# Input statistics, the conv's last chunk and a split inverse in a hand-ordered WKV and graph-conv kernel

## The chip, the cores and the metric

The kernel runs on one core of one Trainium2 chip. The time is the device time of one launch in microseconds (us), given as the median of the runs. Each engine of a core (TensorE, VectorE, ScalarE, GpSimd, and SyncE, which here only issues DMAs) works through its own queue in order. Engines wait for one another through semaphores.

## The reference

The input x has 16 images of 192 channels and 56 x 56 = 3136 positions, in float32. Three WKV layers and a graph convolution follow one another. Each takes the group norm of x (32 groups) and adds its result to x.

```python
def _L0_conv_ref(x, Wk, Wv, Wr, Wo, ln_g, ln_b, w_decay, u):
    k, v, r = xs @ Wk.T, xs @ Wv.T, xs @ Wr.T            # over positions t
    x_fwd = wkv_scan(-exp(w_decay), u, k, v)
    x_bwd = flip(wkv_scan(-exp(w_decay), u, flip(k), flip(v)))
    h = sigmoid(r) * 0.5 * (x_fwd + x_bwd)
    h = (h - mean(h)) * rsqrt(var(h) + 1e-5) * ln_g + ln_b   # over channels
    return h @ Wo.T
def _L3_conv_ref(x, conv_w, ...):
    x_j = max(roll(x, +-2, rows) - x, roll(x, +-2, columns) - x, 0)
    y = conv_w @ concat([x, x_j]) + conv_b
    return gelu(batch_norm(y))
for layer in (L0, L1, L2, L3): x = x + layer(_gn(x))
```

(The code above is shortened. The scan is a quotient of two decaying sums along t, one weighted by exp(k) and one by exp(k) times v, with a bonus u for the current position.)

## The kernel before, in words

**Tiles.** Two images make a pair, and there are 8 pairs. A pair's 2 x 192 channels are laid on 128 partitions as three rows j = 0, 2, 1 (two full ones and one that holds 64 channels of each image), which the kernel always takes in this order. The 3136 positions are cut into 7 chunks of 448 columns. So a tile is 128 x 3 x 448, most operations come in three instructions of 128x448, and operations on a whole tile have 1344 columns. All these tiles live in 33 slots of SBUF. A slot that is given back goes to the end of a list, and the next one is taken from its front (`Slot`, L501 to L509). A slot that was given back a moment ago may still have a reader under way, and its next writer then waits for it. [...]

**Units of work.** A WKV layer of a pair has 7 forward units A (chunks 0 to 6) and then 7 backward units B (chunks 6 to 0). A conv of a pair has 7 units C.
- A: product k (`a_keys`) and its exponential into `ek` (`a_exp`); product v (`a_values`); `ekv` = v times ek (`a_ekv`, L908); a scan of ek into `den` (`a_q`) and of ekv into `h` (`a_p`), each three instructions at L855; the bonus terms `a_den` and `a_num` (L870, one instruction of 896 columns and one of 448); the inverse of den as exp(-ln(den)) on ScalarE (`ln` L933, `exp_minus` L936); and `a_y` (L940), GpSimd's product of h with it, after which den's slot is given back. For chunks 0 and 6, `a_y` ends with small products into `chk` (L946, L948).
- B: product r (`b_gate`), exponential (`b_exp`) and sigmoid; backward scans `b_q` and `b_p`; `b_den`, `b_num`; the inverse; nine GpSimd products and sums (`b_mix`, L996 to L998); squares (L1005), sums over channels on TensorE (`b_sums`), the row of deviations (`b_rs1`, `b_rs2`, `b_rs3`), its spread over the partitions (`b_spread`, L1036), `b_scale` (L1041), the output product (`b_out`), the sum with x (`b_x`, L1054) and its store, and the statistics of the new x for the next group norm (`b_stats`).
- C: maxima over rows and columns on VectorE (`c_rows`, `c_columns`, L1080 to L1096), products of x and of the maxima (`c_product`, halves 0 and 1, "cv" in the profile), and Gelu with two table loads, sum and store (`c_end`, `store`).
- Z: statistics of a pair's input, needed by its first layer's norm: two ScalarE instructions per row (L724, L725; each is followed by a read of the accumulator), six per chunk (`chunk_stats`).

**Order.** All engines' queues are written out by hand. Pairs go in two streams (even and odd). A list of 249 steps (L1165 to L1200), numbered from 0 here, puts the B units of one stream beside A or C units of the other. In the list's third column stands the Z unit of a step. Functions by kind of step issue the instructions: `both_a` (B beside A), `both_a_first` (the same, in the first step of six), `both_c` (B beside C), `forward_a` and `forward_c` (one unit alone), and `backward_alone`. What a B unit still has to do after its step is remembered in `late` as a stage (0, 0.5, 1, 2), and the next steps pick it up. Unfinished group norms are four parts in `norms`; each `gap()` issues one.

The stretches that the text speaks of are these:
- Steps 0 to 6 are pair 0's A units alone. Steps 8 to 13 have B of pair 0 beside A of pair 1, and step 14 is A6 alone.
- From step 15 on, layers alternate in the same way (B6 alone, six steps of both, A6 alone, 8 steps in all) up to the conv.
- Steps 48 to 53 are `both_c` (B of pair 1's last layer beside C of pair 0). Then comes a **lone stretch**: A0 of pair 2, C6 of pair 0, A1 to A6 of pair 2 (steps 54 to 61). There are six of these, in steps 54 to 61, 69 to 76, 116 to 123, 131 to 138, 178 to 185 and 193 to 200.

Before, Z units of pair p + 1 are counted in the steps in which pair p's first layer runs forward (L1203 to L1205). These are steps 0 to 6 for pair 1, steps 8 to 14 for pair 2, and the first five lone stretches for pairs 3 to 7. The chunk is loaded at the step's start, and its six ScalarE instructions stand at the step's end.

Of the kernel before, what the change touches and what calls it, by code (L numbers as in the profile page):

```python
# [34 lines left out]
F32 = mybir.dt.float32  # L35
# [438 lines left out]
def fast_path(ctx: ExitStack, tc: tile.TileContext, flag, x, wproj, wfold, wcfold, wconst, wgroup, sums, picks, vecs, out):  # L474
# [9 lines left out]
    small = ctx.enter_context(tc.tile_pool(name="fsmall", bufs=4))  # L484
    dram = ctx.enter_context(tc.tile_pool(name="fdram", bufs=1, space=bass.MemoryType.DRAM))
# [220 lines left out]
    class Run:  # L706
        def __init__(self, pr, l, stats, src=None, first=None):
            self.pr, self.l, self.stats, self.src = pr, l, stats, src
            self.xa, self.xb, self.xz = {}, {}, {}
            if first is not None:  # L710
                self.xa[0] = first
            self.begun, self.before = False, None
            self.bias, self.ps = {}, {}
            self.ek, self.ekv, self.h, self.den, self.sg, self.rs = {}, {}, {}, {}, {}, {}
            self.m, self.ml, self.q, self.p = {}, {}, {}, {}

    def new_stats():
        return small.tile([P, 2, 3, NL], F32, tag="stats", name=name("stats"))

    def chunk_stats(stats, xt, c, whole=False):  # L720

        for j in ORDER:
            if not whole:
                S.activation(junk, xt[:, j, :], AF.Identity, accum_out=stats[:, 0, j, c : c + 1])  # L724
            S.activation(junk, xt[:, j, :], AF.Square, accum_out=stats[:, 1, j, c : c + 1])  # L725
# [154 lines left out]

    def a_keys(run, c):
        product(run, "k", run.w[0], run.xa[c], c == 0)
        slot_of(run.ek, c, "ek")
        if c == 0:
            take_bias(run, "k", S)

    def a_exp(run, c, js):
        ps, e = run.ps["k"], run.ek[c]
        for j in js:
            S.activation(e.t[:, j, :], ps[j][:, 0:L], AF.Exp, bias=run.bias["k"][:, j, :])  # L890
            release(ps[j])

    def a_values(run, c):
        xs = run.xa.pop(c)
        product(run, "v", run.w[1], xs, c == 0)
        if c == NL - 1:

            run.xb[c] = xs
            mean_column(run, xs)
        else:  # L900
            xs.give()
# [9 lines left out]
    def a_q(run, c):  # L911
        run.den[c] = scan(run, "q", run.ek[c], AHEAD, c == 0)

    def a_save(run, c):
        if c < NL - 1:
            save(run.den[c], AHEAD, slot_of(run.ek, c + 1, "ek"), S)
        else:
            run.last = stile("cvb")
            S.activation(run.last, run.den[c].t[:, :, L - 1 : L], AF.Copy)  # L919
# [6 lines left out]
    def a_den(run, c):  # L926
        bonus(run, run.den[c], run.ek[c], run.den[c])

    def a_num(run, c):
        bonus(run, run.h[c], run.ekv[c], run.h[c])  # L930

    def ln(s):
        S.activation(s.t, s.t, AF.Ln)  # L933

    def exp_minus(s):
        S.activation(s.t, s.t, AF.Exp, scale=-1.0)  # L936

    def a_y(run, c):
        den = run.den.pop(c)
        G.tensor_mul(run.h[c].t, run.h[c].t, den.t)  # L940
        den.give()
        if c in (0, NL - 1):
            edge, grow = params[run.l][2:4]
            chk = run.chk[:, 3 * NL : 3 * NL + 9].rearrange("p (k j o) -> p k j o", k=3, o=1)
            col = 0 if c == 0 else L - 1
            G.tensor_mul(chk[:, 1 if c == 0 else 2], run.ek[c].t[:, :, col : col + 1], edge)  # L946
            if c == NL - 1:
                G.tensor_mul(chk[:, 0], run.last, grow)  # L948

# [195 lines left out]
    def z_stats(run, c):  # L1145
        xs = run.xz.pop(c)
        chunk_stats(run.stats, xs.t, c)
        xs.give()
# [3 lines left out]
    for pr in range(npairs):  # L1152
        runs = [Run(pr, 0, new_stats() if pr < 2 else None)]
        for l in range(NLAYERS):
            runs[-1].follow = Run(pr, l + 1, None)
            runs[-1].follow.before = runs[-1]
            runs[-1].dst = [dram.tile([P, 3, L], F32, tag=f"x{pr}_{l}_{c}", name=name("xd")) for c in range(NL)]
            runs.append(runs[-1].follow)
        chains.append(runs)
# [43 lines left out]
    for pr in range(1, npairs):  # L1203
        for c in range(NL):
            steps[at[pr - 1, 0, c]][2] = ("Z", chains[pr][0], c)  # L1205
    starts = {}
    for pr in range(npairs):
        counted = at[pr - 1, 0, NL - 1] + 1 if pr > 0 else 0
        starts.setdefault(max(counted, at[pr, 0, 0] - 2), []).append(chains[pr][0])
# [16 lines left out]
    def deviation(u):  # L1226
        b_rs1(*u)
        b_rs2(*u)
        b_rs3(*u)
        late[u] = 1  # L1230
# [26 lines left out]
    def both_a(b, a, nback, nfront):  # L1257
# [19 lines left out]
        invert(b[0].ek[b[1]])  # L1277
# [13 lines left out]
        a_save(*a)  # L1291
        exp_keys(nfront, (0, 2))
        b_squares(*b, (2,))
        exp_keys(nfront, (1,))
        b_squares(*b, (1,))
        b_sums(*b)
        a_p(*a, S)
        gap()
# [53 lines left out]
    def both_c(b, a, nback, nfront):  # L1352
# [45 lines left out]
        if l0:  # L1398
            spread_and_scale(l0)
        c_end(*a, False)  # L1400
        late[b] = 0

    def forward_a(a, nback, nfront):
# [5 lines left out]
        ahead = nfront is not None and nfront[1].begun  # L1409
        if ahead:  # L1410
            load_ahead(nfront)
# [3 lines left out]
        if l:  # L1415
# [12 lines left out]
            if ahead:  # L1428
                keys(nfront)
                exp_keys(nfront)  # L1430
# [4 lines left out]
            gap()  # L1435
        else:
            if l2:
                add(l2)
            if ahead:
                keys(nfront)  # L1440
            a_ekv(*a)
            if ahead:
                exp_keys(nfront)
            a_p(*a, S)
            if l0:
                squares_and_sums(l0)
                b_rs1(*l0)
                late[l0] = 0.5
            a_den(*a)
            invert(den())  # L1450
            a_num(*a)
            gap()
# [6 lines left out]
        if not ahead:  # L1459
            load_ahead(nfront)  # L1460
            keys(nfront)
            exp_keys(nfront)

    def forward_c(a, nback, nfront):
# [3 lines left out]
        if ahead:  # L1468
            load_ahead(nfront)
        c_product(*a, 0)  # L1470
        c_rows(*a)
        if h:
            b_rs2(*h)
            b_rs3(*h)
        c_columns(*a)
        store()
        if h:
            b_spread(*h)
            b_scale(*h)
# [66 lines left out]
    with tc.manual_schedule(engines={PE.engine, V.engine, S.engine, G.engine, nc.sync.engine}):  # L1546
# [6 lines left out]
        for i, (b, f, z) in enumerate(steps):  # L1553
# [6 lines left out]
            if z is not None:  # L1560
                if z[1].stats is None:
                    z[1].stats = new_stats()
# [3 lines left out]
            if f and not b and i + 2 < len(steps):  # L1566
                if nfront is not None and nfront[0] == "A" and steps[i + 2][1] is not None:
                    far = steps[i + 2][1]
                    if far[1] is nfront[1]:
                        load_ahead(far)  # L1570
            if b and f and f[0] == "A":
                (both_a if of_stage(0) is None else both_a_first)(b[1:], f[1:], nback, nfront)
            elif b and f:
                both_c(b[1:], f[1:], nback, nfront)
            elif f:
                (forward_a if f[0] == "A" else forward_c)(f[1:], nback, nfront)
# [7 lines left out]
        assert not late and not unsummed  # L1584
# [98 lines left out]
```

## Time and profile before

| what | value |
|---|---|
| median of 3 runs (lowest, highest) | 5327.02 us (5325.39, 5331.32) |
| profiled execution's own time | 5330.99 us |
| its span | 5329.2 us |
| granted TensorE clock in it | 0.919 |
| DVE busy | 4891.2 us (92%) |
| PE busy | 4607.2 us (86%) |
| ACT busy | 3701.4 us (69%) |
| POOL busy | 2750.7 us (52%) |
| an ordinary step of both halves (429.5 to 454.5) | 25.0 us, DVE busy 24.94 |
| a lone stretch with Z (1259.8 to 1388.3) | 128.5 us, DVE busy 98.4 |

The profile calls the engines PE (TensorE's matmuls), PEld (its weight loads), DVE (VectorE), ACT (ScalarE), POOL (GpSimd) and SPq (SyncE's queue of DMA issues). A busy PE is not a PE at its peak. A step's time is read on DVE, from the end of its last bonus term to that of the next step. A group or a timeline line is named by the tiles that it writes and reads ("p<-p,q": h from h and den; buffer names are those of the scans, so h appears as p and den as q).

### The profile page before, as it was taken

What the parts mean: (1) busy time and instruction counts of PE and PEld (TensorE: products, weight loads), DVE (VectorE), ACT (ScalarE), POOL (GpSimd) and SP (SyncE); (2) the same over time, 40 slices, a digit from 0 to 9 for tenths busy, and PEclk for the clock granted to TensorE, in tenths of its full rate; (3) what the DMA queues carried; (4) which work ended last, traced back from release to release, by engine and by line L of the source; (5) the groups of instructions that cost most, each with busy time, mean ns of one, the idle gap of its engine ahead of it and who ended that gap; (6) DMA issues with size and microseconds to landing.
All of it is one profiled execution on the core that took longest, in us unless ns stands there. A gap on an engine that the chain in (4) does not pass through costs nothing.

```text
span 5329.2 us, 51050 instructions
## 1 busy us (share of the span) xinstructions
PE 4607.2 (86%) x15206; PEld 1484.5 (28%) x15206; DVE 4891.2 (92%) x6460; ACT 3701.4 (69%) x7114; POOL 2750.7 (52%) x2109
## 2 busy tenths in 40 slices
PE   6789988988788898898888889988888888898897
PEld 2222222222222222222222222222222322232222
DVE  6799999997989999999797999999979799999995
ACT  6777777766766777777676777777757567777672
POOL 1455555654454565555354456555635355565562
PEclk8889999989899999999889999999998999999898
DMA  5222222134233222123424221222343312122233
GB/s 150 78 75 78 85 77 78 68 101 134 82 117 96 77 80 77 70 78 121 130 79 136 70 75 68 86 75 81 114 124 104 98 57 75 66 82 80 78 107 112
DMA packets 314270, 482.41 MB, mean 91 GB/s; under 512 B 66432, under 2 KB 306688, under 8 KB 313984
## 3 DMA queue, kind: packets, MB, share of 16 engines
q1 hardware_dynamic: 312832, 477.59, 28.1%
q8 instruction: 123, 2.02, 0.2%
q10 hardware_dynamic: 1152, 1.48, 0.1%
q14 instruction: 163, 1.34, 0.1%
HBM read 324.83 MB, written 154.14 MB: 90 GB/s over the span
## 4 chain that ended last, share of the span: by engine, by line
DVE 52%; PE 28%; ACT 7%; POOL 6%; issue 5%; DMA 2%; SPq 0%; DVEq 0%; POOLq 0%; ACTq 0%
DVE p L855 13%; DVE q L855 10%; DVE q L870 5%; DVE ek L870 4%; DVE ekv L908 3%; DVE p L1041 3%; DVE p L870 3%; DVE ekv L870 3%; DVE x L1054 2%; PE ops L592 2%; PE st L1014 2%; PE ops L594 2%; PE ops L593 2%; PE rsb L1036 2%; POOL p L998 2%
## 5 line engine op out<-in xcount | busy, mean ns | idle before, releaser
L940 POOL TENSOR_TENSOR p<-p,q 128x1344 f32<-128x1344 f32 x168 | 512.5, 3051 | 1173.1 <-ACT q L936 875.4
L855 DVE TENSOR_TENSOR_SCAN q<-fdecays,ek 128x449 f32<-128x449 f32 (+1 forms) x1008 | 1024.6, 1071 | 51.5 <-ACT ek L890 33.4
L855 DVE TENSOR_TENSOR_SCAN p<-fdecays,ekv 128x449 f32<-128x449 f32 (+1 forms) x1008 | 1024.4, 1072 | 5.2 <-POOL p L940 1.9
L996 POOL TENSOR_TENSOR ekv<-ekv,ek 128x448 f32<-128x448 f32 x504 | 617.9, 1226 | 712.5 <-DVE p L1041 299.2
L998 POOL TENSOR_TENSOR p<-p,sg 128x448 f32<-128x448 f32 x504 | 610.7, 1212 | 64.2 <-ACT sg L936 17.3
L997 POOL TENSOR_TENSOR p<-p,ekv 128x448 f32<-128x448 f32 x504 | 601.5, 1194 | 39.5
L890 ACT ACTIVATE ek<-k,k 128x448 f32<-128x448 f32 x504 | 294.3, 631 | 388.3 <-PE k L595 352.8
L1036 PE MATMUL rsb<-rs,fpicks 32*128 32x448 f32 (+1 forms) x1008 | 369.2, 644 | 127.4 <-ACT rs L1030 127.4
L1005 ACT ACTIVATE ek<-p 128x448 f32<-128x448 f32 x504 | 282.9, 572 | 265.6 <-POOL p L998 264.8
L725 ACT ACTIVATE fjunk<-x 128x448 f32<-128x448 f32 x672 | 387.6, 577 | 64.1 <-issue 24.0
L592 PE MATMUL ops<-p,fwo 128*128 128x448 f32 x336 | 222.5, 752 | 210.7 <-DVE p L1041 210.7
L870 DVE SCALAR_TENSOR_TENSOR q<-ek,fcc,q 128x896 f32<-128x896 f32 x336 | 388.0, 1195 | 3.4 <-ACT cvb L919 2.9
L1054 DVE SCALAR_TENSOR_TENSOR x<-ops,fwob,x 128x448 f32<-128x448 f32 x504 | 315.1, 673 | 57.7 <-PE ops L595 45.3
L870 DVE SCALAR_TENSOR_TENSOR ek<-ek,fcc,q 128x896 f32<-128x896 f32 x336 | 359.4, 1111 | 9.2 <-POOL chk L946 9.2
L908 DVE SCALAR_TENSOR_TENSOR ekv<-v,v,ek 128x448 f32<-128x448 f32 x504 | 313.8, 677 | 43.2 <-PE v L595 35.5
L724 ACT ACTIVATE fjunk<-x 128x448 f32<-128x448 f32 x600 | 343.3, 572 | 13.1
L1041 DVE TENSOR_TENSOR p<-p,rsb 128x448 f32<-128x448 f32 x504 | 282.4, 615 | 75.6 <-PE rsb L1036 75.6
L961 ACT ACTIVATE sg<-r,r 128x448 f32<-128x448 f32 x504 | 313.0, 628 | 16.9 <-PE r L595 10.8
L870 DVE SCALAR_TENSOR_TENSOR ekv<-ekv,fcc,p 128x896 f32<-128x896 f32 x336 | 320.7, 996 | 1.2
L870 DVE SCALAR_TENSOR_TENSOR p<-ekv,fcc,p 128x896 f32<-128x896 f32 x336 | 297.2, 925 | 2.9 <-ACT ekv L864 2.8
L1123 POOL TENSOR_TENSOR ml<-ml,x 128x1344 f32<-128x1344 f32 x56 | 178.5, 3187 | 221.5 <-ACT ml L1117 221.5
L933 ACT ACTIVATE q<-q 128x1344 f32<-128x1344 f32 x168 | 223.0, 1327 | 98.1 <-DVE q L870 85.3
(234 smaller groups left out, 11386.5 us busy)
## 6 DMA issues: line engine op xcount, KB each, us to landing
x<-xd SPq DMA_DIRECT2D x240, 672.0 KB, 5.7
xd<-x SPq DMA_DIRECT2D x168, 672.0 KB, 3.9
x<-in_x_dram SPq DMA_DIRECT2D x320, 224.0 KB, 4.4
x<-in_x_dram SPq DMA_DIRECT2D x320, 112.0 KB, 4.5
out_dram<-ml SPq DMA_DIRECT2D x112, 224.0 KB, 2.3
ring<-xd SPq DMA_DIRECT2D x112, 168.0 KB, 5.5
wkv<-in_wfold_dram SPq DMA_DIRECT2D x24, 640.0 KB, 5.4
out_dram<-ml SPq DMA_DIRECT2D x112, 112.0 KB, 2.3
```

The source lines that it names most:

```text
L724: S.activation(junk, xt[:, j, :], AF.Identity, accum_out=stats[:, 0, j, c : c + 1])
L725: S.activation(junk, xt[:, j, :], AF.Square, accum_out=stats[:, 1, j, c : c + 1])
L855: V.tensor_tensor_scan(out, dec[:, column(j)].to_broadcast([P, L if first else L + 1]), e, 0.0, ALU.mult, ALU.add)
L870: by_channel(lambda js, i: V.scalar_tensor_tensor(dst.t[:, js, :], e.t[:, js, :], cc[:, i : i + 1], state.t[:, js, :], ALU.mult, ALU.add))
L908: V.scalar_tensor_tensor(e.t[:, j, :], ps[j][:, 0:L], b[:, j, :], run.ek[c].t[:, j, :], ALU.add, ALU.mult)
L940: G.tensor_mul(run.h[c].t, run.h[c].t, den.t)
L996: G.tensor_mul(y.t[:, j, :], y.t[:, j, :], den.t[:, j, :])
L997: G.tensor_add(h.t[:, j, :], h.t[:, j, :], y.t[:, j, :])
L998: G.tensor_mul(h.t[:, j, :], h.t[:, j, :], sg.t[:, j, :])
L1036: PE.matmul(ps[j][:, :L], pick[rows, j, :], rs[rows, :], start=True, stop=True)
L1041: V.tensor_mul(h[:, j, :], h[:, j, :], ps[j][:, :L])
L1054: V.scalar_tensor_tensor(xj, ps[j][:, 0:L], wob[:, column(j)], xj, ALU.add, ALU.add, accum_out=run.new[:, 0, j, c : c + 1] if c == 0 else ...
```

## The change

**Statistics of the input.** Z units go into steps with both a B and an A unit whose step before also has a forward unit (`full`): for each pair the last seven free ones ahead of its first layer. Where there are too few (pair 1), they stay where they were. In `both_a` the six instructions are issued in three parts of two (`count`). A new pool `counts` holds the statistics.

**Conv's last chunk.** In the last step of `both_c`, A0's scan `a_q` and product `a_values` are issued ahead of and beside `b_scale`. `forward_c` for C6, if an A follows and a B unit waits at stage 0.5, issues only the maxima of C6, with that B unit's deviation, spread, scale and output product, and with the keys, scan and values of the next A. Its two products go to a list `convs`, from which `forward_a` takes one in each of the next steps that has no b_x to add (A2 and A3). `forward_a` gets a branch for stage 0, takes the keys of the next A even if C6 lies between, and loads the chunk after the next.

**Inverse.** In `both_a` the backward inverse is issued as ln and exp of rows 0 and 2 and then ln and exp of row 1.

**Order of chk.** The small products into `chk` move from `a_y` to `a_den`.

```diff
-    def z_stats(run, c):
-        xs = run.xz.pop(c)
-        chunk_stats(run.stats, xs.t, c)
-        xs.give()
+    def z_stats(run, c, js=ORDER):
+        if run.stats is None:
+            run.stats = input_stats()
+        chunk_stats(run.stats, run.xz[c].t, c, js=js)
+        if js[-1] == ORDER[-1]:
+            run.xz.pop(c).give()
...
-    for pr in range(1, npairs):
-        for c in range(NL):
-            steps[at[pr - 1, 0, c]][2] = ("Z", chains[pr][0], c)
+    full = [i for i, (b, f, _) in enumerate(steps) if b and f and f[0] == "A" and steps[i - 1][1] is not None]
+    counted_by = {}
+    for pr in reversed(range(1, npairs)):
+        ends = [i for i in full if i < at[pr, 0, 0] - 2 and steps[i][2] is None][-NL:]
+        if len(ends) < NL:
+            ends = [at[pr - 1, 0, c] for c in range(NL)]
+        for c, i in enumerate(ends):
+            assert steps[i][2] is None
+            steps[i][2] = ("Z", chains[pr][0], c)
+        counted_by[pr] = ends[-1] + 1
...
     def both_a(b, a, nback, nfront, z):
+        def count(j):
+            if z is not None:
+                z_stats(*z[1:], (j,))
...
         b_den(*b)
-        invert(b[0].ek[b[1]])
+        for js in (AC, slice(1, 2)):
+            ln(b[0].ek[b[1]], js)
+            exp_minus(b[0].ek[b[1]], js)
...
         a_save(*a)
+        count(0)
         exp_keys(nfront, (0, 2))
         b_squares(*b, (2,))
         exp_keys(nfront, (1,))
+        count(2)
         b_squares(*b, (1,))
         b_sums(*b)
         a_p(*a, S)
+        count(1)
         gap()
         a_den(*a)
...
     def both_c(b, a, nback, nfront):
...
-        if l0:
+        ahead = nback is None and l0 and nfront is not None and nfront[0] == "A"
+        if ahead:
+            a_q(*nfront[1:])
+            a_save(*nfront[1:])
+            b_spread(*l0)
+            c_end(*a, False)
+            a_values(*nfront[1:])
+            b_scale(*l0)
+            b_out(*l0)
+            late[l0] = 2
+        elif l0:
             spread_and_scale(l0)
-        c_end(*a, False)
+        if not ahead:
+            c_end(*a, False)
...
+    def conv_part():
+        if convs:
+            u, half = convs.pop(0)
+            c_product(*u, half)
+            if half == 1:
+                c_end(*u, False)
...
     def forward_a(a, nback, nfront, nkeys):
...
+        elif l0:
+            a_den(*a)
+            invert(den())
+            a_ekv(*a)
+            b_squares(*l0)
+            a_p(*a, S)
+            b_sums(*l0)
+            if ahead:
+                keys(nkeys)
+            a_num(*a)
+            b_rs1(*l0)
+            late[l0] = 0.5
+            if ahead:
+                exp_keys(nkeys)
+            if l2:
+                add(l2)
+            sum_up(1)
...
         else:
             if l2:
+                a_den(*a)
+                invert(den())
                 add(l2)
-            if ahead:
-                keys(nfront)
+            else:
+                conv_part()
             a_ekv(*a)
             if ahead:
-                exp_keys(nfront)
+                keys(nkeys)
+                exp_keys(nkeys)
+            gap()
             a_p(*a, S)
...
     def forward_c(a, nback, nfront):
...
+        if h and ahead and nfront[0] == "A":
+            c_rows(*a)
+            b_rs2(*h)
+            b_rs3(*h)
+            c_columns(*a)
+            store()
+            b_spread(*h)
+            keys(nfront)
+            exp_keys(nfront)
+            b_scale(*h)
+            a_q(*nfront[1:])
+            a_save(*nfront[1:])
+            a_values(*nfront[1:])
+            b_out(*h)
+            late[h] = 2
+            convs.extend(((a, 0), (a, 1)))
+            return
```

`a_keys`, `a_exp`, `a_values`, `a_q` and `a_save` note what they have issued (`once`), so a unit's part that came early isn't issued again in its own step.

## The prediction

> **What bounds the kernel now.** I read the busy shares first, then the stages, then the gaps of VectorE in each stage. On the page:
>
> ```profile
> PE 4607.2 (86%) x15206; PEld 1484.5 (28%) x15206; DVE 4891.2 (92%) x6460; ACT 3701.4 (69%) x7114; POOL 2750.7 (52%) x2109
> ...
> DVE 52%; PE 28%; ACT 7%; POOL 6%; issue 5%; DMA 2%; SPq 0%; DVEq 0%; POOLq 0%; ACTq 0%
> ```
>
> DVE is the bound, and only its 438 us of idle time (5329.2 - 4891.2) can be won. The table of busy time by stretch says where they are (columns: length, then PE, PEld, DVE, ACT, POOL):
>
> ```profile
> 156.60:357.60 201.00, 168.46 (x519) 52.20 (x518) 168.78 (x208) 146.61 (x302) 100.59 (x78) 0.85 0.23 73
> 372.30:545.10 172.80, 156.47 (x514) 49.23 (x514) 170.13 (x204) 127.18 (x235) 100.66 (x80) 0.91 0.18 61
> ...
> 2570.50:2699.10 128.60, 106.10 (x318) 35.54 (x314) 98.46 (x142) 75.42 (x158) 34.48 (x18) 0.89 0.41 115
> 4167.50:4292.20 124.70, 107.13 (x319) 35.74 (x318) 97.65 (x142) 52.77 (x86) 38.15 (x21) 0.90 0.30 86
> ```
>
> Line 1 is steps 8 to 14, both halves with the counting of pair 2's input ("Z"); line 2 is the same work one layer on, without Z: 28.2 us less. Line 3 is a lone stretch (a pair's first layer forward with the last conv chunk in it, steps 116 to 123): DVE works 98.5 of 128.6 us. There are six such stretches; line 4 is the last, which has no Z: 3.9 us less. An ordinary step of both halves takes 25.0 us with 24.94 of DVE: nothing to win, and any delay there is lost.
>
> DVE's order in time, in a lone stretch, then in step 11 (Z), then in step 168 (no Z); brackets hold the idle time before and its releaser:
>
> ```profile
> 2574.11 1.69 DVE L1041 TENSOR_TENSOR p<-p,rsb 128x448 f32<-128x448 f32 x3 [3.65 <-PE rsb L1036]
> ...
> 2607.91 1.15 DVE L1041 TENSOR_TENSOR p<-p,rsb 128x448 f32<-128x448 f32 x2 [5.21 <-PE rsb L1036]
> ...
> 2614.69 3.06 DVE L855 TENSOR_TENSOR_SCAN q<-fdecays,ek 128x449 f32<-128x449 f32 x3 [4.03 <-ACT ek L890]
> 2623.04 0.68 DVE L1054 SCALAR_TENSOR_TENSOR x<-ops,fwob,x 128x448 f32<-128x448 f32 x1 [5.28 <-PE ops L595]
> ```
> ```profile
> 259.09 3.06 DVE L855 TENSOR_TENSOR_SCAN q<-fdecays,ek 128x449 f32<-128x449 f32 x3 [5.57 <-POOL p L940]
> ```
> ```profile
> 3629.83 3.04 DVE L855 TENSOR_TENSOR_SCAN q<-fdecays,ek 128x449 f32<-128x449 f32 x3
> 3632.91 0.63 DVE L1024 TENSOR_TENSOR rs<-st,rs 64x448 f32<-64x448 f32 x1
> 3633.57 3.06 DVE L855 TENSOR_TENSOR_SCAN p<-fdecays,ekv 128x449 f32<-128x449 f32 x3
> ```
> ```profile
> 3631.70 3.06 POOL L940 TENSOR_TENSOR p<-p,q 128x1344 f32<-128x1344 f32 x1 [5.00 <-ACT q L936]
> ```
>
> The wait in step 11 isn't one for data: the backward q-scan writes a new slot, and POOL's L940 (a_y) reads the old `den` just before that slot is given back. The Z chunk takes one more slot, so the first-in-first-out list of free slots is down to its newest entry. Without Z the q-scan starts at once.
>
> [...] a 16-column maximum at L1094 (0.17 us elsewhere) took 3.05 us beside L940's 3.07 at 2596.40.
>
> **The change, part by part.**
>
> *Z leaves steps 8 to 14.* They should become line 2: -28.2 us. It stays in steps 0 to 6, where DVE has no gap.
>
> *Chk before a_den.* The page's waits show DVE L870 (b_den) behind POOL L946: 9.2 us, 6 times, since L946 stood behind L940. Now it stands ahead: -9.
>
> *The lone stretch.* I re-time steps 115 to 123 from 2570.46 (end of b_num) with durations of this stretch: scan triple 3.05, bonus pair 1.75, ekv triple 1.85, b_x triple 1.85, b_scale 1.7, a product 4.58 on PE, rsb 1.97, sums 2, psg 2.6, one counted chunk on ACT 4.2 (6 x 0.70).
> The q-scan of A0 now fills the gap before b_scale: scan to 2573.5, b_scale 2574.1 to 2575.75, a_den to 2577.45. On PE v follows rsb, but two of its banks come from the conv's Gelus (2576.4), so v ends 2580 and ops 2584.6. DVE: ekv to 2582, p-scan 2585, a_num 2586.75, b_x 2588.6. ACT: squares 2582.8, rs1 2587.1, keys' exponentials 2591.8, b_stats of one chunk 2596, then b_rs3 2597.3. DVE: c_rows and rs2 2590.9, c_columns (5.9 without the collision with L940) 2596.8; rsb lets b_scale start 2598.4 (1.6 idle), q-scan of A1 2603.1, a_den 2604.8. PE: rsb 2599.3, v 2603.9, ops 2608.5; b_x thus ends 2609.2 (2.1 idle), ekv 2611, p-scan 2614, a_num 2615.8, where the kernel before is at 2636.4. That is 20.6 us earlier. Then PE is the later one: k 2613.1, v 2617.7, conv half 2622.3, k 2626.9, psg 2629.5, v 2634, conv half 2638.6, k 2643.4 (behind the Gelus). DVE: A2 to 2627.3, A3 to 2641.2 (1.7 idle), A4's scan starts 2644 (2.5 idle), and at four chunks x 11 to 11.5 A6 ends near 2678.5 against 2699.1. So -20.6 for five stretches, and 3.9 less for the last, which had no Z: -119.7 together. Bounds: surely gone are Z's 3.9 (five times) and the 3.65 before b_scale (six times), 41 in all; all the idle time, 30.1 of line 3, would be 180 less Z's part. I keep 119.7: the two halves of the conv cost 9.2 us on a PE that is then almost full.
>
> *Inverse in two parts.* ACT: 128x1344 takes 1.33, 128x448 0.57, so 128x896 about 0.95: 3.05 instead of 2.66 per step; the first exp ends at 3639.6 instead of 3641.0, so POOL starts 1.35 us earlier. No DVE instruction waits for it in these steps: 0 (cover: ACT's 5.8 us of slack in 25).
>
> *Z goes into 42 steps of both halves* (14 for each two pairs). No DVE instruction is added, but 4.2 us of ACT and a slot. Three stretches of 2 x 0.70 enter ACT's queue: count(0) falls in a 2.89 us gap ahead of the keys' exponentials; count(2) holds up the last square (and PE's sums, then r, v, rsb, by 1.55), count(1) the row's square rs1 and a_den's ln. In step 167 rs1 starts at 3653.41; with the counts squares end 3653.8, the p-save 3654.0, count(1) 3655.4: rs1 and ln come 2.0 us later, and so a_y. As for the slot, I followed the list by hand. At a step's start it has six, the newest being den. Loads of Z and two other chunks, sg and the q-scan take five; **the backward p-scan gets den's slot** and waits for a_y. (Z is given back ahead of den, so q is spared, p isn't.) p starts 3.74 us after q (fence), and a_y ends 1.19 after p's start today (3634.76 against 3633.57); in other steps of the kind 0.63 or 1.5. With a_y 2.0 later after a Z step: stalls of 0.7 to 1.6 in a first Z step, 2.7 to 3.3 in the next. It applies where two other chunks are loaded: steps 26, 27, 33, 34, 35, 41, 42, 43, in sum 0.75+3.3+1.6+2.7+3.3+1.6+2.7+3.3 = 19.3. The nine steps after the other Zs wait about 0.5 for rsb (1.55 late, slack about 1): 4.5. Three groups of two pairs: +71. Bounds: 0 (if slots don't bind and PE's slack holds) and 5.7 x 42 = 239 (what a Z step cost in step 10: 30.7 against 25.0).
>
> *DMAs.* The Z loads (4 of 0.5 us each on SP) move with their steps; SP is idle at a step's start, and the chunk is needed some 15 us on. Other loads come earlier only. 0.
>
> Sum: -28.2 - 9 - 119.7 + 71.3 = -85.6. On the profiled execution (5330.99; span 5329.2 and 1.8 around it) 5245.4; it stands 4 above the median, so **5241** for the median of 5327.0.
>
> **Rivals.** *Hidden counts*: if the p-scan's slot is old enough, no part of the 71 is paid: 5327 - 157 = 5170. Against it stands the step 11 wait. *PE holds the lone stretch*: PE shows 106 busy of 128.6; if only the certain 41 come: -41-28-9+71 = -7, 5320. Against: [...]the stretch needs about 20 products of 4.58. *Slower: Z steps cost what they cost in step 10*, by slot waits on a_y: 239 - 157 = +82, 5409. It decides from 157/42 = 3.7 us a step. For it: the same load, the same list, the only precedent; against: q's wait becomes p's, with 3.7 us of cover.
>
> **Chances.** Forecast 0.62 (own range 5200 to 5285), hidden counts 0.18, PE 0.10, slower 0.10. About 0.2% (10.7 us) is what a measurement can tell from no change. Faster 0.84 (the first two and 0.04 of PE's), same 0.06, slower 0.10. The range takes all but the slower rival and tails: 5168 to 5316.
>
> **What would show it.** Steps 8 to 14 near 172; a lone stretch near 108, with gaps before L1041 and L1054 of 1 to 2.5; b_den no longer behind L946; in the Z steps a gap before the p-scan ended by POOL L940, of about 3 us, in 8 of 14. If those gaps are missing, it is the first rival; if every Z step is near 30, the third; if lone stretches stay above 120, the second.

## Result and profile after

The changed kernel takes 5288.15 us (median of 4 runs, 5287.25 to 5291.86) against 5327.29 for the kernel before (4 runs, 5325.39 to 5331.32): a ratio of 0.9927, 95% interval 0.991 to 0.9944. It is 39 us faster; the forecast was 86 us. The profiled execution took 5287.25 us, its span 5285.4.

The page of the changed kernel, busy time and the chain's shares by engine:

```profile
PE 4589.5 (87%) x15206; PEld 1469.0 (28%) x15206; DVE 4859.7 (92%) x6460; ACT 3715.8 (70%) x7284; POOL 2781.3 (53%) x2109
...
DVE 46%; PE 26%; ACT 9%; POOL 8%; issue 7%; DMA 3%; SPq 0%; DVEq 0%; POOLq 0%; ACTq 0%
```

DVE is still the bound, but two things moved that a chain of shares doesn't separate. Its busy time fell by 31.5 us (4891.2 to 4859.7), though the number of its instructions is the same; its idle time fell only from 438.0 to 425.7. The forecast was all idle time.

Busy time by stretch in the changed kernel (length, then PE, PEld, DVE, ACT, POOL), for steps 8 to 14, the lone stretch of steps 116 to 123, and the last lone stretch:

```profile
156.20:326.60 170.40, 153.65 (x520) 48.29 (x518) 167.03 (x207) 124.64 (x239) 101.23 (x80) 0.93 0.20 61
2554.20:2675.40 121.20, 101.61 (x318) 32.88 (x316) 100.72 (x143) 52.56 (x86) 35.91 (x20) 0.93 0.27 83
4142.80:4262.30 119.50, 103.31 (x316) 33.83 (x314) 99.99 (x141) 52.47 (x86) 38.17 (x23) 0.90 0.28 84
```

Steps 8 to 14 came to 170.4 us, as foreseen (172). The lone stretch came to 121.2 where 108 was foreseen, although DVE works only 100.7 of it. To see the whole, I split both traces into steps (on DVE, from the end of a step's last bonus term to that of the next) and added them up by kind:

| kind of step (number) | before, us | after, us | change | DVE idle | DVE busy |
| --- | --- | --- | --- | --- | --- |
| 8 to 14, Z gone (7) | 201.0 | 170.4 | -30.6 | -28.8 | -1.8 |
| lone stretches (48) | 767.1 | 721.3 | -45.8 | -59.9 | +14.1 |
| B6 behind a lone stretch (6) | 65.1 | 62.3 | -2.8 | -9.2 | +6.4 |
| both halves, Z new (42) | 1053.6 | 1120.1 | +66.5 | +91.5 | -24.9 |
| both halves, no Z (38) | 954.9 | 929.1 | -25.8 | -0.7 | -25.1 |
| all others (107) | 2271.1 | 2266.3 | -4.8 | -4.7 | -0.1 |

So there is a gain that the prediction didn't have (DVE's busy time in the steps with both halves), a loss of about the size foreseen, and lone stretches with 74 us too little gain (45.8 for 119.7). The waits of DVE in the changed kernel (waiting line, line waited for: us in all, times, longest):

```profile
DVE p L875 <- ACT ekv L869: 110.8, 58, 10.3
DVE p L860 <- POOL p L967: 45.4, 24, 2.3
```

The second line is the foreseen one: the backward p-scan (L860) waits 24 times, 8 for each two pairs, for a_y (L967, before L940) to let go of den's slot. The first was not foreseen: a_num (L875) writes over p in place and must wait until ACT has copied p's last column (L869). Six of the 58 are waits of 8.2 to 10.3 us; DVE's order in time in the stretch shows where (in brackets the idle time ahead):

```profile
2582.80 1.15 DVE L1061 TENSOR_TENSOR p<-p,rsb 128x448 f32<-128x448 f32 x2 [1.03 <-PE rsb L1056]
...
2593.36 0.69 DVE L1074 SCALAR_TENSOR_TENSOR x<-ops,fwob,x 128x448 f32<-128x448 f32 x1 [3.16 <-PE ops L596]
...
2639.18 1.75 DVE L875 SCALAR_TENSOR_TENSOR p<-ekv,fcc,p 128x896 f32<-128x896 f32 x2 [10.13 <-ACT ekv L869]
```

The gap before b_scale (L1061) has shrunk to the foreseen size (1.03, and 0.64 before its third row, for 1.6). That before b_x (L1074) has not quite: 3.16, and 0.57 before its third row, for 2.1. A new one of 10 us stands in A3. ACT's copy is queued behind the exponentials of A4's keys, those wait for PE's product, and PE waits for its input:

```profile
PE k L593 <- DMA x<-in_x_dram: 7.3, 1, 7.3
```

Why the input is late stands in the queue of SyncE, here in order of time, and then its longest wait there:

```profile
2595.95 0.58 SPq L1079 DMA_DIRECT2D xd<-x  x1
2623.68 0.33 SPq L797 DMA_DIRECT2D wkv<-in_wcfold_dram  x1
2624.07 0.58 SPq L831 DMA_DIRECT2D ring<-xd  x1
2624.70 0.61 SPq L832 DMA_DIRECT2D ring<-xd  x1
2625.35 0.61 SPq L542 DMA_DIRECT2D x<-in_x_dram  x1
```
```profile
SPq L797 <- PE cv L602: 27.1, 1, 27.1
```

SyncE issues nothing for 27 us (2596.5 to 2623.7). `sum_up` in A1 begins the next run (`begin_later`), which asks for its weights (L797, or L800 if a layer is next). The pool has two buffers for them; the older holds the old conv's weights, and the change has put that conv's second half into A3. The loads of ring (the edges of a conv chunk's neighbours) and input behind it in the queue needed none of that.

### The profile page after: what moved, and what is told of

The parts are those of the page before. It is cut to its first block, busy times and chain, and to the rows that moved or that the text cites. A ratio compares the mean times of both kernels' runs of the same rounds, so it can differ in the third digit from the quotient of the medians.

```text
span 5285.4 us, 51409 instructions
## 1 busy us (share of the span) xinstructions
PE 4589.5 (87%) x15206; PEld 1469.0 (28%) x15206; DVE 4859.7 (92%) x6460; ACT 3715.8 (70%) x7284; POOL 2781.3 (53%) x2109
## 3 DMA queue, kind: packets, MB, share of 16 engines
q1 hardware_dynamic: 312832, 477.59, 28.2%
q14 instruction: 167, 1.37, 0.1%
## 4 chain that ended last, share of the span: by engine, by line
DVE 46%; PE 26%; ACT 9%; POOL 8%; issue 7%; DMA 3%; SPq 0%; DVEq 0%; POOLq 0%; ACTq 0%
DVE p L860 11%; DVE q L860 9%; DVE ek L875 3%; DVE ekv L875 3%; DVE p L875 3%; DVE q L875 3%; DVE ekv L925 3%; DVE p L1061 3%; POOL p L1018 2%; POOL p L967 2%; DVE x L1074 2%; PE ops L593 2%; POOL ekv L1016 2%; PE ops L595 2%; POOL p L1017 2%
## 5 line engine op out<-in xcount | busy, mean ns | idle before, releaser
L967 POOL TENSOR_TENSOR p<-p,q 128x1344 f32<-128x1344 f32 x168 | 511.8, 3047 | 1288.4 <-ACT q L963 893.3
L860 DVE TENSOR_TENSOR_SCAN p<-fdecays,ekv 128x449 f32<-128x449 f32 (+1 forms) x1008 | 1025.2, 1074 | 47.9 <-POOL p L967 45.4
L860 DVE TENSOR_TENSOR_SCAN q<-fdecays,ek 128x449 f32<-128x449 f32 (+1 forms) x1008 | 1025.8, 1075 | 9.2 <-ACT ek L905 7.9
L1017 POOL TENSOR_TENSOR p<-p,ekv 128x448 f32<-128x448 f32 x504 | 599.9, 1190 | 39.5
L1056 PE MATMUL rsb<-rs,fpicks 32*128 32x448 f32 (+1 forms) x1008 | 354.0, 619 | 98.4 <-ACT rs L1050 98.4
L875 DVE SCALAR_TENSOR_TENSOR p<-ekv,fcc,p 128x896 f32<-128x896 f32 x336 | 295.7, 923 | 110.8 <-ACT ekv L869 110.8
L875 DVE SCALAR_TENSOR_TENSOR ek<-ek,fcc,q 128x896 f32<-128x896 f32 x336 | 365.7, 1130 | 0.0
L875 DVE SCALAR_TENSOR_TENSOR q<-ek,fcc,q 128x896 f32<-128x896 f32 x336 | 360.7, 1117 | 2.2 <-ACT ek L869 1.7
L1074 DVE SCALAR_TENSOR_TENSOR x<-ops,fwob,x 128x448 f32<-128x448 f32 x504 | 315.2, 677 | 48.8 <-PE ops L596 29.2
L875 DVE SCALAR_TENSOR_TENSOR ekv<-ekv,fcc,p 128x896 f32<-128x896 f32 x336 | 320.8, 997 | 1.2
L1061 DVE TENSOR_TENSOR p<-p,rsb 128x448 f32<-128x448 f32 x504 | 282.3, 616 | 36.5 <-PE rsb L1056 36.5
L960 ACT ACTIVATE ek<-ek 128x896 f32<-128x896 f32 (+1 forms) x253 | 237.4, 939 | 77.8 <-DVE ek L875 51.4
```

Source lines behind the costliest of these rows:

```text
L860: V.tensor_tensor_scan(out, dec[:, column(j)].to_broadcast([P, L if first else L + 1]), e, 0.0, ALU.mult, ALU.add)
L875: by_channel(lambda js, i: V.scalar_tensor_tensor(dst.t[:, js, :], e.t[:, js, :], cc[:, i : i + 1], state.t[:, js, :], ALU.mult, ALU.add))
L960: S.activation(s.t[:, js, :], s.t[:, js, :], AF.Ln)
L1017: G.tensor_add(h.t[:, j, :], h.t[:, j, :], y.t[:, j, :])
L1056: PE.matmul(ps[j][:, :L], pick[rows, j, :], rs[rows, :], start=True, stop=True)
L1061: V.tensor_mul(h[:, j, :], h[:, j, :], ps[j][:, :L])
```

## Experiments

All ran beside the kernel before; each ratio is to it, with its 95% interval. Where nothing was changed, most groups of steps differ by up to 4 us between runs, and the 18 other single backward steps by up to 14 (253.6 to 267.4 us in all), so only clearly larger differences are read.

**Lone stretches: the queue.** The next conv's weights are held back until the old conv's second half is issued:

> The changed kernel, but the next conv's weights are asked for only after the old conv's second half has been issued on PE, in the step A3 (in the changed kernel SyncE asks for them in A1 and stands 27 us, since their buffer is still to be read by that half, and the loads of A4's input stand behind it). My theory: the idle 8.4 to 10.3 us of VectorE in A3 of each of the six lone stretches come from that queue. Then the wait of PE's k product for its input (7.3 us) and that of a_num for ACT's copy (10 us) go, each lone stretch falls from about 120 to about 111 us, and the kernel from 5288 to about 5238 us (5230 to 5255). Rival: TensorE's two conv halves fill A2 and A3 anyway, and a product of k is late with or without the load; then each stretch stays above 117 us and the kernel between 5270 and 5290.

```diff
+        if run.l == NLAYERS and convs:
+            held.append(run)
...
             if half == 1:
+                while held:
+                    run = held.pop(0)
+                    kv = wpool.tile([P, 2, FCOLS], F32, tag="kv", name=name("wkv"))
+                    nc.sync.dma_start(kv, wcfold)
+                    run.weights = kv, None
                 c_end(*u, False)
```

Measured: 5267.94 us (0.9885, 0.987 to 0.990). Three stretches fell to 111.5 to 112.3 us (A3's idle time 0.5 us), three stayed at 117.9 to 119.5. In those SyncE still stood 27.1 us, for a layer's weights. So all weights were held back:

> The changed kernel, but whichever weights are next (the conv's or a layer's) are asked for only after the old conv's second half has been issued on PE in A3. Holding back the conv's weights alone took A3's idle time on VectorE from 8.5, 10.3 and 10.5 us to 0.5 in three of the six lone stretches and left 7.7, 9.4 and 9.2 in the others; there, I think, it is the layer's weights that stand in SyncE's queue. My theory: now all six stretches come to 111 to 112.5 us, and the kernel, 5268 with three of them, falls by another 3 x 8 us to about 5244 (5238 to 5252). Rival: in the other three stretches the k product is late for another reason, a slot for A4's input; then they stay near 119 and the kernel near 5268.

Measured: 5236.09 us (0.9828, 0.9814 to 0.9841), 52 us less than the changed kernel; the lone stretches took 666.4 us in all, each about 111. SyncE in the same stretch of this kernel, then DVE at the end of A3:

```profile
2580.53 0.58 SPq L1085 DMA_DIRECT2D xd<-x  x1
2581.20 0.57 SPq L837 DMA_DIRECT2D ring<-xd  x1
...
2588.22 0.58 SPq L545 DMA_DIRECT2D x<-in_x_dram  x1
2608.26 0.33 SPq L805 DMA_DIRECT2D wkv<-in_wcfold_dram  x1
```
```profile
2614.01 1.75 DVE L881 SCALAR_TENSOR_TENSOR p<-ekv,fcc,p 128x896 f32<-128x896 f32 x2 [0.37 <-ACT ekv L875]
```

The ring and the input are asked for at once; the weights' own DMA still comes only after the conv's product, and that is early enough. a_num's gap is 0.37 us. The rivals (PE full, a missing slot) fall.

With the queue free a stretch still takes 111 us where 108 was foreseen. The missing 3.1 us lie before the end of A1, in b_spread's matmuls (tile rsb) and the product v behind them. Here is rsb in the stretch before the change and after it:

```profile
2605.94 3.72 PE L1036 MATMUL rsb<-rs,fpicks 32*128 32x448 f32 x6 [8.40 <-ACT rs L1030]
```
```profile
2580.83 3.65 PE L1056 MATMUL rsb<-rs,fpicks 32*128 32x448 f32 x6 [6.08 <-ACT rs L1050]
```

Rsb starts 26.6 us into the stretch (26.8 foreseen), behind 6.08 us in which PE was idle. With the queue free the gap ahead of it is the same, 6.1 us. Rsb then takes 3.65 us for the 1.97 put in, and v takes 6.3 for 4.58; the granted clock over the two is 0.64. The output product behind them, and with it b_x, come 3 us late. In the kernel before, the same place had shown 3.72 us behind a gap of 8.40.

**Lone stretches: the new order by itself.** Everything of the change but the new order of the conv's last chunk and the steps around it:

> The changed kernel with the lone stretches' steps (the conv's last chunks and a pair's first chunks) in the order of the kernel before; the counting, the check product and the two-part inverse stay changed. My theory: the new order as it stands, with SyncE's queue stopped, is worth only the 46 us measured in the stretches, of which about 20 (3.9 in five of six) came of the counting having left them; so the old order costs 26 us: about 5314 us (5306 to 5322), with A3's long idle time gone and no 27 us stop of SyncE. With the queue free (the kernel that held all weights back, 5236) the same order is worth 78. Rival: half of the two edits' gain is the counting's; then under 5300.

Measured: 5321.35 us (0.9985, 0.9978 to 0.9991); the stretches took 747.7 us. The new order is worth 26 us in them as it stands, and 81 (747.7 to 666.4) with the queue free. The counting that left five of the six gave the other 19.4 (767.1 to 747.7), as foreseen (5 x 3.9).

**The inverse in two parts.** Undone in the changed kernel, then done alone in the kernel before, in `both_a` only:

```diff
-        for js in (AC, slice(1, 2)):
-            ln(b[0].ek[b[1]], js)
-            exp_minus(b[0].ek[b[1]], js)
+        invert(b[0].ek[b[1]])
```

> The changed kernel with the backward inverse in one part again (one Ln and one Exp over all three thirds). The prediction costed the two parts at 0. My theory from the two traces: they start GpSimd's three b_mix products 1.3 us earlier, so that GpSimd's last products no longer lie beside VectorE's a_den, whose 896-wide part fell from 1622 to 1117 ns; undone, that part returns to about 1600 ns, an ordinary step with both halves goes from 24.4 back to about 25.0 us, and the kernel rises by 80 x 0.63 = 50 us to about 5338 us (5320 to 5345). Rival: the shorter a_den comes of something else in the change (the check product's new place): then the part stays near 1120 ns and the kernel within 10 us of 5288.

> The kernel before, with nothing but the backward inverse in two parts in the steps with both halves. The prediction costed this at 0. Undoing it in the changed kernel cost 39.5 us, 25.8 of them in the 38 steps with both halves that don't count. My theory: the three b_mix products end earlier and so lie less beside VectorE's a_den; the part is worth the same alone, in 80 steps of 0.63 us: 5328 - 50 = 5278 us (5272 to 5290). Rival: it needs a_den's later start, which comes with the other parts of the change (the check product ahead of it, or the counting); alone it gives less than 10 us: above 5318.

Measured: undone 5327.68 us (0.9999, 0.999 to 1.0007), so 39.5 more; alone 5273.72 us (0.9899, 0.9884 to 0.9914), **55 less than the kernel before**. One part that was costed at nothing is worth more alone than the whole change. (The first expectation set the mean of one width beside that of a mixed group; the groups' busy times below are the like figures.) The line of a_den, q<-ek,fcc,q, on the pages of before, after, after with the inverse undone, and before with it alone (busy us, mean ns):

```profile
L870 DVE SCALAR_TENSOR_TENSOR q<-ek,fcc,q 128x896 f32<-128x896 f32 x336 | 388.0, 1195 | 3.4 <-ACT cvb L919 2.9
```
```profile
L875 DVE SCALAR_TENSOR_TENSOR q<-ek,fcc,q 128x896 f32<-128x896 f32 x336 | 360.7, 1117 | 2.2 <-ACT ek L869 1.7
```
```profile
L875 DVE SCALAR_TENSOR_TENSOR q<-ek,fcc,q 128x896 f32<-128x896 f32 x336 | 413.1, 1269 | 2.2 <-ACT ek L869 1.7
```
```profile
L870 DVE SCALAR_TENSOR_TENSOR q<-ek,fcc,q 128x896 f32<-128x896 f32 x336 | 338.7, 1050 | 3.2 <-ACT cvb L919 2.6
```

The same 336 instructions take 388 or 339 us. In time, step 168 of the kernel before, POOL and then DVE:

```profile
3674.36 1.15 POOL L997 TENSOR_TENSOR p<-p,ekv 128x448 f32<-128x448 f32 x1
3675.59 1.13 POOL L998 TENSOR_TENSOR p<-p,sg 128x448 f32<-128x448 f32 x1
```
```profile
3675.90 2.36 DVE L870 SCALAR_TENSOR_TENSOR q<-ek,fcc,q 128x896 f32<-128x896 f32 x2
```

and with the inverse in two parts, same step:

```profile
3629.46 1.15 POOL L998 TENSOR_TENSOR p<-p,sg 128x448 f32<-128x448 f32 x1
```
```profile
3630.60 1.73 DVE L870 SCALAR_TENSOR_TENSOR q<-ek,fcc,q 128x896 f32<-128x896 f32 x2
```

POOL's last product ended 0.8 us after a_den's start and now ends as a_den starts: 2.36 becomes 1.73. That it is POOL's work, and not something else about the inverse, was tried by leaving out POOL's three products for the last third of the channels:

> The kernel before, leaving out GpSimd's three mixing products of the last third of the channels in the steps with both halves (so that third isn't mixed). It takes GpSimd's work away from beside VectorE's a_den and changes nothing on VectorE or ACT before it. My theory: a_den (q from ek and q, all three operands in SBUF) is slow only where GpSimd works beside it (2.0 to 2.5 us instead of 1.13 for its 896-wide part); with the third left out the 336 instructions fall from 401 us in all to 355 or less, and an ordinary step with both halves from 25.0 to 24.3 us; the kernel to about 5270 us. Rival: a_den is slow for its own reason; then it keeps its 401 us.

Measured (one execution): 5272.54 us; the line reads 336.2 us, 52 less than before (instruction by instruction, as the expectation counts: 401.5 to 350.8). The inverse was left alone there, and the whole effect came. In the changed kernel the split inverse takes 26 us of busy time off the 42 counting steps too, but 21 of them come back there as waits (idle time 94.1 us with it, 72.8 with it undone), so it is worth less there than alone. (The 896-wide part of a_den took 1.75 us in most of these steps of the kernel before, not the 2.0 to 2.5 of the expectation.)

**Z steps: the slot.** In the 42 steps the counted chunk is loaded after the backward p-scan has taken its slot:

```diff
-            if z is not None:
+            if z is not None and not (b and f and f[0] == "A" and of_stage(0) is None):
                 load_ahead(z)
...
         b_p(*b)
+        load_ahead(z)
         b_den(*b)
```

> The changed kernel, but in the 42 steps that count, the counted chunk's four loads are asked for after the backward scan of p instead of at the step's start; so that scan gets the slot that the counted chunk takes now. My theory: the scan's 24 waits for GpSimd's y (45.4 us) are the slot's, and go to about 0; the kernel falls to about 5248 us (5240 to 5262), the waits of a_num (about 52 of 1 us) staying. Rival: the loads then wait for the late slot, SyncE stands, and what is queued behind it or the counting on ACT is late: the scan's waits go but the gain is under 15 us (5275 to 5295).

Measured: 5231.21 us (0.9816, 0.9803 to 0.983), 57 less than the changed kernel. The p-scan's waits are gone, and the 42 steps fell by 68.1 us, to 1051.9: more than the 45.4 of the waits. Part of a_num's waits went along, though ACT does the same work. The chain is in step 27, PE's order in the changed kernel and with the late load:

```profile
614.13 1.02 PE L593 MATMUL ops<-p,fwo 128*128 128x448 f32 x2 [2.82 <-DVE p L1061]
614.99 1.63 PE L594 MATMUL ops<-p,fwo 128*128 128x448 f32 x2
```
```profile
610.77 1.02 PE L593 MATMUL ops<-p,fwo 128*128 128x448 f32 x2 [0.98 <-DVE p L1061]
611.62 0.91 PE L594 MATMUL ops<-p,fwo 128*128 128x448 f32 x2
```

The scan's wait leaves PE idle for 2.82 us instead of 0.98, and the product that follows is slow. The busy time of the 6.5 us around it has the granted clock as its third figure from the end, ahead of the DMA share and GB/s (changed kernel, then late load):

```profile
613.50:620.00 6.50, 5.87 (x14) 1.79 (x14) 6.50 (x11) 5.21 (x16) 6.19 (x6) 0.74 0.00 0
```
```profile
610.50:617.00 6.50, 6.23 (x20) 2.17 (x20) 6.50 (x10) 5.58 (x17) 6.19 (x6) 1.00 0.00 0
```

0.74 against 1.00. The product takes 6.2 us instead of 4.6, k behind it comes 1.6 us late, and so do the exponentials, the squares and ACT's copy. To separate this from ACT's two extra passes, PE was kept busy behind the wait:

> The changed kernel with two matmuls of no use (128x448 into a spare half bank of PSUM, about 1.9 us of PE) behind the spreading of the deviation in the 24 counting steps in which the backward scan of p waits for its slot. In step 27 of the changed kernel that wait (2.3 us on VectorE) left PE idle for 2.8 us, and the product that followed took 6.1 us instead of 4.6, at a granted clock of 0.76; so k's product, ACT's exponentials and ACT's copy of p came 1.5 us later still, and a_num waited 1.1 us. My theory: the slot wait costs more than itself by that; with PE kept busy the product takes 4.6 us again, a_num's waits in these steps go (about 24 x 1.1 us) while p's slot waits stay, and the kernel falls to about 5265 us (5255 to 5275). Rival: the a_num waits come of ACT's two more passes alone; then the product is shorter but the kernel stays within 5 us of 5288.

Measured: 5444.35 us (1.0217, 1.0203 to 1.023). It told nothing: p's scan, which reads its decays beside the matmuls' target, waited 8 us for them in each of the 24 steps. With a bank of their own (PSUM's banks are handed out from a list of seven, `bank`, L513):

```diff
+    def keep_busy():
+        spare = bank("spare")
+        for _ in range(2):
+            PE.matmul(spare[:, 0:L], gmat[:, 0:P], gmat[:, 0:L], start=True, stop=True)
+        release(spare)
...
             b_spread(*l)
+        if busy:
+            keep_busy()
         b_p(*b)
```

> As busy_pe, but the two useless matmuls write to a bank of PSUM that is free at that point, not beside the decays that VectorE's scans read (there the backward scan of p waited 8 us for them, 24 times, and the comparison was lost). What is to be seen: in the 24 steps with the slot wait the product ops after it takes 4.6 us instead of 6.1. My theory: a_num's waits in those steps are the slot wait's second half, by way of TensorE's lower clock; they go, and the kernel falls from 5288 to about 5265 us (5255 to 5275), p's slot waits (45 us) staying. Rival: a_num waits for ACT's two more passes alone; then the product is shorter, but a_num's 110.8 us of waits stay above 100 and the kernel within 5 us of 5288.

Measured: 5251.25 us (0.9854, 0.9838 to 0.9871): **two matmuls of no use in 24 steps make the kernel 37 us faster**. Step 27 on PE (a matmul stands as two records):

```profile
610.38 1.77 PE L1294 MATMUL spare<-fgmat 128*128 128x448 f32 x4
613.36 0.99 PE L593 MATMUL ops<-p,fwo 128*128 128x448 f32 x2 [1.21 <-DVE p L1061]
614.19 0.91 PE L594 MATMUL ops<-p,fwo 128*128 128x448 f32 x2
```

and DVE's waits in this kernel:

```profile
DVE p L875 <- ACT ekv L869: 82.5, 35, 10.0
DVE p L860 <- POOL p L967: 38.5, 24, 2.2
```

The product is no longer slow: its first two pairs of records take 0.99 and 0.91 us, where the changed kernel had 1.02 and 1.63. The slot's 24 waits stay (38.5 us), a_num's fall from 58 to 35: in the 24 steps all of its 24 waits (28.3 us) are gone, while in the other 18 counting steps its 9 waits (14.9 us) stay. So those 24 were the slot wait's second half, by way of TensorE's clock (0.74 in step 27 of the changed kernel); the 9 are not.

**Z steps: ACT's copy.** Two edits went at a_num's wait directly: the second third of the counting behind the copy, and the copy on DVE itself.

> The changed kernel, but the second third of the counting (two passes on ACT) stands behind ACT's copy of p's last column instead of ahead of the squares. My theory: a_num, which writes over p, waits for that copy in the counting steps (58 waits in all, 110.8 us, of which about 57 us lie in the 42 counting steps' group and the rest in A3 of the lone stretches); with the copy two passes (1.15 us) earlier nearly all of the 1 us waits go, and the kernel falls to about 5243 us (5235 to 5260). Rival: the four passes that now stand together ahead of the inverse of den make GpSimd's y later by about 0.6 us a step, and p's slot wait takes the gain over: a_num's waits go, but those of the p scan rise by as much, and the kernel stays between 5275 and 5295.

> The changed kernel, but in the 42 counting steps VectorE itself copies the last column of p (three elements a partition) right behind the scan, instead of ACT behind two counting passes. Moving those passes instead made the kernel 15 us slower. My theory: a_num's waits for that copy in the counting steps (about 54 us of the 110.8) go, for about 42 x 0.1 us of copies; but a counting step's y on GpSimd starts no earlier, since the inverse of den on ACT sets it, and so the slot wait of p stays (45 us) or grows by what VectorE is now ahead, up to 1 us in each of its 24 steps. So 5288 - 54 + 4 + 12 to 24, about 5255 (5240 to 5270). Rival: every step is set by ACT's queue, VectorE only waits elsewhere: other waits take all of it over, and the kernel stays above 5280.

Measured: 5302.74 us (0.9952, 0.9938 to 0.9965), 15 *more* than the changed kernel, and 5280.70 us (0.991, 0.9895 to 0.9926), 7 less. Both my theories fell, for the same reason: a_num's waits in the counting steps did go (43.2 us before, 4.1 us and none now; in all 58 became 41 and 27), but p's slot waits rose to 51 us, and DVE, coming earlier, met POOL's products: a_den's line gained 14.5 and 7.7 us, and the 16 A6 steps 12.4 and 12.6. Where the counting was moved, the backward q-scan also came to wait for it (13.4 us). Both edits treated the symptom.

**Together.** Weights held back, late load, and DVE's copy; then without the copy:

> The changed kernel with three of these edits together: all next weights held back until the conv's second half, the counted chunk's loads behind the backward scan of p, and VectorE's own copy of p's last column in the counting steps. If each takes away its own wait and no other comes in its place: 5231 (late loads alone) - 45 (six stretches) - 35 (a_num's 92.3 us of waits in that run less the 57 in A3) + 4 (copies) = about 5155 us (5145 to 5175). If in the counting steps the copy's wait is only exchanged for another of ACT, it stays at about 5186 to 5195.

> The changed kernel with two of the three edits of the best so far (5174): all next weights held back, and the counted chunk's loads behind the backward scan of p; ACT keeps the copy of p's last column. If the two add: 5231 - 52 = 5179 us (5172 to 5186), so that VectorE's own copy is worth about 5 us. Rival: the copy only moved the loss into the single forward steps (they took 12.7 us more with it); then this kernel is as fast or faster: below 5172.

Measured: 5174.24 us (0.9714, 0.970 to 0.9727) and 5175.71 us (0.971, 0.9697 to 0.9723). The two edits add up to within 4 us of what each gave; the copy adds nothing that can be told apart. Either is **154 us faster than the kernel before** and 113 faster than the change as it was.

## Why the prediction was right or wrong

- *Z leaves steps 8 to 14*, -28.2: measured -30.6, of it 28.8 idle time. Right.
- *Chk before a_den*, -9: the wait is gone (9.2 us of idle time), but in those six steps DVE's busy time rose by 6.4, so the steps gained 2.8. The traces show where: b_den, which no longer waits until POOL's a_y has ended, now runs beside it and takes 2.88 to 2.94 us for 1.75, in all six. It is the same overlap as with the split inverse, with the other sign.
- *The lone stretch*, "-119.7 together": measured -45.8. **This is the step that failed**, and with it "*DMAs* ... Other loads come earlier only. 0." I re-timed PE, ACT and DVE through the stretch and put the conv's second half on PE at 2638.6 without asking who waits to write what it reads: the weights of the next run, asked for in A1, with every load after A1 behind them on SyncE. That cost 55 us (721.3 to 666.4 with the queue free). Of the rest, 19 us, each stretch lacks about 3.1 up to the end of A1 (17.5 gained for 20.6 in the one shown). There the durations failed, "a product 4.58 on PE, rsb 1.97": behind a gap of 6.1 us they were 6.3 and 3.65. (a_den of A0 also took 3.00 us instead of 1.7, beside POOL, but rsb started in time all the same.) The rival "PE holds the lone stretch" had the sign in part (three stretches above 120, three at 119.4 to 119.6) but not the cause: PE's two halves fit. A slip in the same sum: from 2644 to 2678.5 are three chunks of 11.5, not four; the end stands.
- *Inverse in two parts*, 0: worth 55 us alone and 39.5 within the change. The step "no DVE instruction waits for it" asked only for waits. The prediction itself had the trace line that bears on it (the 16-column maximum that took 3.05 us beside L940, and 0.17 elsewhere), and had POOL's 1.35 us in hand; it didn't look what DVE runs when POOL's last product ends.
- *Z in 42 steps*, +71.3: measured +66.5, but as the sum of +91.5 idle and -24.9 busy from the inverse. That the total came so close is luck: 71.3 was meant as idle time, and the gain from the inverse hid the excess. The mechanism was right to the count (24 waits, 8 in 14 steps); of the eight single steps, five came within 0.8 us and three were 1.2 to 1.3 us longer. Idle time per step in the first group of 14, us:

| step | 26 | 27 | 33 | 34 | 35 | 41 | 42 | 43 | the six others |
| --- | --- | --- | --- | --- | --- | --- | --- | --- | --- |
| foreseen | 0.75 | 3.3 | 1.6 | 2.7 | 3.3 | 1.6 | 2.7 | 3.3 | 4.5 |
| measured | 1.53 | 3.41 | 2.75 | 3.46 | 3.29 | 2.77 | 3.38 | 4.64 | 6.2 |

But its parts were other than thought: in such a step 1.9 us on average are the slot's, and 1.2 more, which I had put down to a longer slot wait, are a_num's by way of TensorE's lower clock (step 27: 0.74, and 1.00 with the late load). The six others wait mostly at a_num for ACT's copy (14.9 us in the three groups), not for rsb as foreseen. (The fence called step 168 in the prediction is of step 167.)

By the step table, the miss adds up: lone stretches +73.9, DVE's busy time in the 38 steps without Z -25.8 (the 25 of the other 42 stand inside the Z term), B6 behind a stretch +6.2, Z -4.8, steps 8 to 14 -2.4, all others -4.8, together +42 on -85.6, which is the -43.4 of the step table (the spans differ by 43.8). The two large errors, the lone stretches and the inverse, had opposite signs, so the total looks better than its parts. The first rival's 5170 is near the 5176 that the kernel has without the queue's and the slot's waits, but by chance: that sum holds nothing of the inverse's gain (50 us in the 80 steps) and is too low by about as much elsewhere: 19 us in the stretches, 6 in the B6 steps and 29 of waits that the counting steps kept.

## What to carry to other kernels

When a read is moved later, ask which write waits for it, which queue that write stands in, and what stands behind it there: a load that must wait for its buffer should be issued when the buffer is free, not when the load is thought of (worth 52 us here). An edit that moves no wait can still move an overlap: list what runs on VectorE while GpSimd reads and writes SBUF, before and after (the 896-wide a_den: 1.14 us alone, 2.35 beside GpSimd). And a wait of a few microseconds on the bounding engine is not its whole price (here 24 waits for the slot brought 28.3 us of others at a_num): look whether TensorE idles behind it and how fast it starts again. A matmul's duration taken from a full stretch didn't hold behind a gap: the product ops took 4.58 us, and 6.03 or more behind 2.5 us.

## What the runs showed of the hardware

- **TensorE after a gap.** In the changed kernel's trace the product ops took 4.58 us (median of 68) where PE had been idle under 1 us, and 6.03 us or more in all 46 cases behind 2.5 us or more; between 1.5 and 2.5 us, 29 of 38 took about 6 or more. The granted clock was 1.00 in each of the 88 products that took under 4.7 us, and 0.59 to 0.76 in the 80 that took over 5.9. Of the gaps of 2.5 us or more, 35 were of 2.5 to 3.4 us and 11 longer; the slow product came behind each.
- **VectorE beside GpSimd.** In the changed kernel the 896-wide a_den took 1.14 us on average where none of GpSimd's tensor operations ran, and 2.35 us (1.5 to 3.1) where they ran over more than 60% of its length (104 and 43 cases). Scans (1.08 and 1.07 us) and operations with one input in PSUM (ekv from v: 0.68 and 0.68; b_scale 0.62 and 0.62) were untouched. B's bonus terms and the maxima, with both tensor inputs in SBUF as a_den has them, took longer on average: the 896-wide b_den 1.13 and 1.37 us, the 896-wide b_num 1.15 and 2.03, the maxima at L1102 0.51 and 3.14.
- **A DMA queue in order.** One weight load that waited for its buffer held up the loads behind it for 27.1 us, six times, with the DMA engines 27% busy in the stretch of steps 116 to 123.
